# Graph attention with a residual layer norm: adjacency pieces ahead of the other loads, table stores from ScalarE's queue, x tiles from SP's, and beta added two iterations later

## The chip, the cores and the metric

The kernel runs on one core of a Trainium2 chip. Its time is the device time in microseconds of that core; the figure quoted for a kernel is the median of several executions. One further execution is taken with the hardware profiler; its time is given beside the span of the trace.

## The reference, cut to what matters

The input x is 8 batches of 2048 nodes with 64 features (float32), adj a sparse 2048 x 2048 integer matrix. Node n has links to the nodes m with adj[n, m] > 0, and to itself. In the inputs low-numbered nodes have the most links.

```python
def _gat_layer(h, mask, b):
    scores = jnp.einsum('...nd,...md->...nm', h, h)
    scores = jnp.where(mask, scores, NEG)
    attn = jax.nn.softmax(scores, axis=-1)
    return jnp.einsum('...nm,...md->...nd', attn, h) + b

mask = graph + jnp.eye(N, dtype=graph.dtype) > 0
h = jnp.einsum('bnc,hdc->bhnd', x, Wh)                    # 4 heads of 64
out_h = _gat_layer(h, mask[None, None], bh[None, :, None, :])
z = leaky_relu(concat of the heads, 0.2)
h2 = jnp.einsum('bnk,dk->bnd', z, Wo)
out2 = _gat_layer(h2, mask[None], bo)
z2 = leaky_relu(out2, 0.2)
out = (z2 - mean) * rsqrt(var + 1e-5) * gamma + beta
x = layernorm(x + out)
```

## The kernel before, in words

The kernel doesn't compute all 2048 x 2048 scores. The first 32 nodes ("hubs") are treated against all nodes. The other 2016 nodes form 168 sets of 12 nodes; for each set the kernel makes a list of up to 128 nodes that any of the twelve is linked to, fetches their rows by an indirect DMA, and computes scores, softmax and weighted sum on that list alone. The first layer takes two sets an iteration, 84 iterations; the second layer follows on rows stored to a second table. A general kernel stands behind a flag for inputs whose lists don't fit; it doesn't run here.

The work falls into three stages.

**The opening**, a loop over 16 tiles of 128 nodes (`for i in range(NB)`, L977). `load_x(i + 4)` (L469) fetches an x tile with two DMAs, four tiles ahead, into one of ten row buffers. `save_x(i)` (L476) stores tile i in the order of the sets to `table1` in DRAM, with one to five DMAs. `hub_scores(i)`, `turn_x(i + 1)` and `hub_values(i - 1)` are the hubs' attention: per tile a subtract on VectorE (L617), an exponential (L619) and a copy of the transposed tile (L607) on ScalarE, in that order.

Beside it the lists are made. The adjacency rows of ten sets are read in two halves; such a half is a *piece*, 120 rows of 1024 integers, and there are 34 (12 for the first 60 sets, 12 for the next 60, 10 for the rest). `more(n)` issues the next n of them by `load_adj` (L686): two or three DMAs on SP's queue (L693, L694) into one of three `raw` buffers, shared at the start with the two halves of the hubs' own rows, then a conversion on GpSimd (L699) into half of a bf16 tile `a`, and after every second piece four or more small selects (L707, L710). The tiles `a` have five buffers, two of which first hold the hubs' mask. `make_keys(r, t, ...)` (L732) turns three tiles `a` into keys by matmuls with powers of two (L741) and two VectorE operations (L730). `make_keys(0, 0)` comes in tile 2, `make_keys(0, 1)` in tile 6, `make_keys(1, 0)` after the loop, behind the last `hub_values`. From the keys of the first round `pick(0)` makes 39 small VectorE jobs, four a tile from tile 6 on, which end in the lists (`index`).

After the loop come `more(2)`, six gathers from `table1` (`gather`, L813, L816, on GpSimd) and `own_rows` (L819, on GpSimd), whose product the next TensorE work (L831) reads.

**The first layer's loop**, `for i in range(-4, NG + 3)` (L1121), written out by hand as a pipeline: scores (L846), masking (L851), exponential (L858), values (L871), the turn back and the projections. In iteration i the rows for i + 5 are gathered. One more piece is issued per iteration (L1163) until they run out.

In iterations 30 to 73 the kernel also prepares x + beta for the end: `load_own(v)` (L938), 12 DMAs on SP's queue (L946) that bring the x rows of eight sets into one of two buffers `xb`, and `add_beta(v)` (L948), which adds beta on GpSimd (L950) and stores the tile to `table3` from SP's queue (L951). Even iterations load, odd ones add what the iteration before loaded. At the end of each iteration `keep_rows` (L917, L922) stores the finished rows of two sets to the second table, also from SP's queue, from one of four row buffers.

**The second layer** (from L1213) fetches rows of the second table and ends in the layer norms and the stores of the output.

The order of instructions on each engine and each DMA queue is the order in which the code issues them. An instruction on GpSimd, or a DMA on a queue, that waits holds all that was issued after it on the same engine.

Of the kernel before, what the change touches and what calls it, by code (L numbers as in the profile page):

```python
# [359 lines left out]
def fast_kernel(ctx: ExitStack, tc: tile.TileContext, x, adj, Wh, bh, Wo, bo, gamma, beta, out, flag):  # L360


    nc = tc.nc
    B, N, C = x.shape
    H, D, _ = Wh.shape
    P = 128
# [37 lines left out]
    def rows_tile(name):  # L404
        return rowp.tile([P, Q, PW], F32, tag="rows", name=name)
# [25 lines left out]
    NV = (NS + 7) // 8  # L431
# [18 lines left out]
    xrow = {}  # L450
# [10 lines left out]
    def in_order(table, a, b):  # L461

        sets = table[HUB:, :].rearrange("(s k) c -> k s c", k=SET)
        runs = [(0, HUB, table[:HUB, :])]
        runs += [(n0, n0 + n, sets[0, s0:s0 + n]) for s0, n0, n in flipped(0, NS)]
        runs += [(HUB + k * NS, HUB + (k + 1) * NS, sets[k]) for k in range(1, SET)]
        return [(max(a, n0), min(b, n1), dst[max(a, n0) - n0:min(b, n1) - n0]) for n0, n1, dst in runs if max(a, n0) < min(b, n1)]

    def load_x(i):  # L469
        t = xrow[i] = rows_tile(f"x{i}")  # L470
        nc.vector.memset(t[:, :, 0:PW:PW - 1], 1.0)
        for p in range(2):
            nc.scalar.dma_start(out=t[:, :, 1 + p * D:1 + (p + 1) * D],
                                in_=x[p::2, i * P:(i + 1) * P, :].rearrange("q n c -> n q c"))

    def save_x(i):  # L476
        for a, b, dst in in_order(table1, i * P, (i + 1) * P):
            nc.sync.dma_start(out=dst, in_=xrow[i][a - i * P:b - i * P].rearrange("n q c -> n (q c)"))

    NCH = HALFN  # L480
    in_round = [min(FIRST, NS - FIRST * r) for r in range(NR)]
# [116 lines left out]
    def hub_columns():  # L598
        py = two("pyh")
        for h in range(H):  # L600
            nc.tensor.matmul(py[:, 0, h * P:(h + 1) * P], gram[:, h, :], xT[:, :, :HUB], start=True, stop=True)
        nc.vector.tensor_copy(yh.rearrange("p (m h) -> p m h", h=H), py[:, 0, :].rearrange("p (h m) -> p m h", h=H))
# [129 lines left out]
    def make_keys(r, t3, new):  # L732

        n = in_round[r]
        groups = [(t, min(S10, n - S10 * t)) for t in range(3 * t3, min(3 * t3 + 3, (n + S10 - 1) // S10))]
        pk = new(f"pk{r}_{t3}")
        for h in range(2):
            c = (2 * t3 + h) * 32
            for b in range(2):
                for i, (t, ns) in enumerate(groups):  # L740
                    nc.tensor.matmul(pk[c:c + 32, b, :], powers_of(ns, t % 3), ahead[r, t][:ns * SET, h, b * 512:(b + 1) * 512],  # L741
                                     start=(i == 0), stop=(i == len(groups) - 1), tile_position=(0, c))
        for h in range(2):
            part = slice((2 * t3 + h) * 32, (2 * t3 + h + 1) * 32)
            keep_keys(keys[r % 2][part, :], pk[part], part, h)
# [192 lines left out]
    def load_own(v):  # L938
        t = xbs[v % 2]
        if v == NV:  # L940
            for q in range(Q):
                nc.sync.dma_start(out=t[q * HUB:(q + 1) * HUB, :2], in_=x[2 * q:2 * q + 2, :HUB, :].rearrange("p n c -> n p c"))
            return
        for k in range(4):
            for part, src in places(x, v, k):
                nc.sync.dma_start(out=t[part].rearrange("p (f w) c -> p f (w c)", f=2), in_=src)  # L946

    def add_beta(v):  # L948
        t = xbs[v % 2]
        nc.gpsimd.tensor_tensor(t, t, bet.unsqueeze(1).to_broadcast([P, 8, D]), OP.add)  # L950
        nc.sync.dma_start(out=table3[v], in_=t.rearrange("p b d -> p (b d)"))  # L951
# [3 lines left out]
    def more(n):  # L955

        for _ in range(n):
            if pieces:
                load_adj(*pieces.pop(0))

    more(2)
    hub_mask()
    hub_mask_sets()
    weights()
    turn_x(0)
    hub_columns()
    picks = []

    def some(n):
# [7 lines left out]
    for i in range(NB):  # L977
        if i + 4 < NB:
            load_x(i + 4)
        more(2 if i < 5 else 0 if i < 8 else 1)  # L980
        save_x(i)
        if i == 2:
            nc.gpsimd.memset(rall[:, NG:, :], 1.0)
            nc.gpsimd.memset(rall2, 1.0)
            nc.gpsimd.memset(over, 0.0)
            for k in range(SET):
                nc.gpsimd.memset(bits[:, k:k + 1], N << k)
            nc.gpsimd.memset(shifts[:, 2:3], EPS)
            nc.gpsimd.memset(ones, 1.0)
            for t in rowts + xbs:  # L990
                nc.gpsimd.memset(t, 1.0)
            if last:
                make_powers6()
        hub_scores(i)
        if i + 1 < NB:
            turn_x(i + 1)
        if i:
            hub_values(i - 1)
        if i in (2, 6):
            make_keys(0, i // 6, two)  # L1000
            if i == 6:
                picks = pick(0)
        some(4)
# [117 lines left out]
    for i in range(-4, NG + 3):  # L1121
        if 0 <= i + 1 < NG:
            sp = one(f"s{i + 1}", "S")
            scores(i + 1, sp)
            weigh(i + 1, sp)
        if i >= 1 and slow and len(slow) % 3:
            slow.pop(0)()
        cat = one(f"cat{i}", "C") if i <= NG else None
        if i < NG:
            ph, pr = cat[:, 0, 384:384 + GM], cat[:GM, 1, 384:512]  # L1130
        else:
            cat = one(f"cat{i}", "S" if i == NG + 1 else "C")
            ph, pr = cat[:, 0, :GM], cat[:GM, 1, :P]
        if 0 <= i - 1 < NG:
            project(held.pop(("ot", i - 1)), cat, GM)
            held["z", i - 1] = leaky(cat, GM, f"z{i - 1}")
        if 0 <= i + 2 < NG:
            t = held["T", 1, i + 2] = work.tile([P, 2, 512], F32, tag="xTg", name=f"xTg{i + 2}", bufs=3)
            for k in range(2):
                nc.scalar.copy(t[:, k, :], bank[k])  # L1140
        if 0 <= i + 1 < NG:
            lift(i + 1)
        if 0 <= i < NG:
            op = one(f"o{i}", "O")
            values(i, op)
            invert(i, op)
        if 0 <= i + LOOK < NG and i > -3:
            for j in range(2):
                gather(table1, 2 * (i + LOOK) + j, 1, rows_tile)
        if NG - LOOK <= i < NG - 1:  # L1150
            for j in range(2):
                k = 2 * (i - NG + LOOK) + j
                hub_block(k, rows_tile(f"gh{k}"))
        if i + 6 < NG and i % 2 == 0 and i >= -2:
            own_rows((i + 6) // 2)
        if i >= 60 and i % 2 == 0 and ahead_of_second:
            ahead_of_second.pop(0)()
        if 0 <= (i - 30) // 2 <= NV:
            (add_beta if i % 2 else load_own)((i - 30) // 2)
        if 0 <= i - 1 < NG:  # L1160
            leak(held["z", i - 1])
        if i >= -3:
            more(1)  # L1163
        if i >= 0:
            if turns():
                some(1)
            if slow and len(slow) % 3 == 0:
                slow.pop(0)()
            if todo3 and i == todo3[0][0]:
                r, part = todo3.pop(0)[1:]  # L1170
                make_keys(r, part, late_two)
                if part:
                    waiting.append(r)
            if not picks:
                ready = done
                if waiting:
                    r = waiting.pop(0)
                    picks = pick(r)
                    done += in_round[r]
            assert i + 1 + LOOK >= NG or 2 * (i + 1 + LOOK) + 1 < ready  # L1180

        if 0 <= i - 2 < NG:
            second_maps(i - 2, ph)
        if 0 <= i - 3 < NG:
            second_rows(i - 3, pr)
        if 0 <= i + 4 < NG + NG % 2:
            columns(i + 4, cat)
        if 0 <= i - 2 < NG:
            keep_own(i - 2, ph)
        if 0 <= i - 3 < NG:  # L1190
            keep_rows(i - 3, pr)
        for _ in range((2 if i < 22 or i % 2 else 1) if i >= 0 else 0):
            if not turns():
                some(1)
        if 0 <= i + 4 < NG + NG % 2:
            keep_columns(i + 4, cat)
        if 0 <= i + 3 < NG:
            turn(bank[0], rows[1, 2 * (i + 3)])
        if 0 <= i < NG:
            turn_values(i, op)  # L1200
            keep_values(i, op)
        if 0 <= i + 3 < NG:
            turn(bank[1], rows[1, 2 * (i + 3) + 1])
        if NG - 3 <= i < NG:
            hub_step(i - NG + 3, bank[0])
# [205 lines left out]
    for u in range(-3, NU + 5):  # L1411
# [12 lines left out]
        if 0 <= u < NU:  # L1424
            a = u % 2
# [10 lines left out]
        if 0 <= u + 1 < NU:  # L1436
            turn_scores(u + 1)
            a = (u + 1) % 2
# [49 lines left out]
```

## Time and profile before

| | |
|---|---|
| median of 3 runs | 898.96 us (896.56 to 905.24) |
| profiled execution | 1030.36 us, span 1028.6 us |
| mean granted TensorE clock in it | 0.924 |
| busy PE, DVE, ACT, POOL | 784.7, 598.0, 507.6, 501.8 us |
| DMA | 125.70 MB, mean 122 GB/s |

PE is TensorE's matmuls, PEld its weight loads, DVE VectorE, ACT ScalarE, POOL GpSimd, SP the engine that only issues DMAs. SPq and ACTq mark what a sequencer did itself, such as issuing a DMA: start, time the issue took, source line. A line of the timeline has the start and the time in us, then engine, source line, operation, output tile<-inputs, shape and count; in brackets stands how long the engine had been idle before it and what ended that. "issue" is time in which the engine waited for nothing that the profile shows. L537 is a helper's line and stands for all transposes of tiles.

### The profile page before, as it was taken

How to read it: one execution, taken by the hardware profiler on the slowest of the kernel's cores; microseconds unless marked ns; L12 is line 12 of the kernel's file. 1: busy time of each engine (PE TensorE's matmuls, PEld its weight loads, DVE VectorE, ACT ScalarE, POOL GpSimd, SP SyncE). 2: the span in 40 equal slices, each digit the busy share in tenths (PEclk: the TensorE clock that was granted, in tenths of full speed). 3: DMA queues.
4: the chain of work that ended last, by engine and by line, in shares of the span. 5: the costliest groups of instructions: out<-in, count | busy, mean ns of one | idle time of the engine just before them, and what ended most of it. 6: DMA issues, size and time to landing. Idle time of an engine off the chain costs nothing.

```text
span 1028.6 us, 42341 instructions
## 1 busy us (share of the span) xinstructions
PE 784.7 (76%) x18079; PEld 675.7 (66%) x18079; DVE 598.0 (58%) x1358; ACT 507.6 (49%) x1038; POOL 501.8 (49%) x709
## 2 busy tenths in 40 slices
PE   3656588999999999898998997319777667677840
PEld 3535477888998888787887886117666555555740
DVE  2339646888777767544555554001467676657793
ACT  2313145655666656555565673005455655555640
POOL 6342756644545555555565532742455565555100
PEclk9978789999999999999999999559899999999975
DMA  7566634432333434344343432953344555544210
GB/s 162 163 198 167 195 102 139 135 81 75 87 89 103 121 110 120 109 113 117 115 114 110 115 96 79 271 143 95 99 119 132 143 150 143 149 138 141 76 52 25
DMA packets 82419, 125.70 MB, mean 122 GB/s; under 512 B 35440, under 2 KB 51672, under 8 KB 82222
## 3 DMA queue, kind: packets, MB, share of 16 engines
q0 software_dynamic: 27168, 69.09, 25.0%
q1 hardware_dynamic: 37922, 49.47, 15.8%
q10 hardware_dynamic: 17132, 4.34, 2.2%
q8 instruction: 145, 2.38, 1.0%
q14 instruction: 52, 0.43, 0.1%
HBM read 124.98 MB, written 18.48 MB: 139 GB/s over the span
## 4 chain that ended last, share of the span: by engine, by line
PE 61%; DVE 12%; issue 9%; ACT 7%; another core or an unknown queue 4%; DMA 3%; SPq 2%; ACTq 1%; POOL 0%; DVEq 0%; POOLq 0%
PE s L846 11%; PE o L871 9%; PE bank L537 7%; PE t L537 6%; PE cat L831 5%; PE cat L556 3%; PE o L888 3%; PE bank L1239 3%; PE cat L905 3%; ACT xts L1384 2%; PE bank L1250 2%; PE o L1269 2%; PE cat L915 2%; DVE var L1319 1%
## 5 line engine op out<-in xcount | busy, mean ns | idle before, releaser
L816 POOL DMA_INDIRECT g<-table,index x168 | 178.4, 1062 | 158.2 <-PE o L871 127.7
L816 POOL DMA_INDIRECT rows<-table,index x168 | 174.0, 1035 | 148.9 <-PE o L1269 88.7
L851 DVE TENSOR_TENSOR e<-s,mask 128x768 f32<-128x768 f32 x84 | 80.4, 957 | 116.7 <-PE s L846 112.8
L846 PE MATMUL s<-y,xTg 64*64 64x48 f32 x5376 | 122.9, 222 | 22.4 <-issue 20.3
L846 PEld LDWEIGHTS s<-y,xTg 64*64 64x64 f32 x5376 | 103.9, 134 | 45.0 <-issue 41.2
L1384 ACT COPY xts<-t 128x1024 f32<-128x1024 f32 x84 | 81.3, 1011 | 82.4 <-PE t L537 43.8
L543 ACT ACTIVATE z<-cat,bhp 128x192 f32<-128x192 f32 x168 | 61.6, 418 | 95.8 <-PE cat L556 94.0
L537 PE MATMUL t<-ident,rows 128*128 128x128 f32 x672 | 93.9, 285 | 14.0 <-issue 13.4
L537 PE MATMUL bank<-ident,g 128*128 128x128 f32 x672 | 102.2, 276 | 0.4 <-DVE keysi L785 0.3
L871 PE MATMUL o<-g,e 128*64 128x65 f32 x2688 | 100.2, 228 | 1.0 <-issue 1.0
L871 PEld LDWEIGHTS o<-g,e 128*64 128x64 f32 x2688 | 88.1, 141 | 11.5 <-issue 2.0
L537 PEld LDWEIGHTS t<-ident,rows 128*128 128x128 f32 x672 | 78.9, 146 | 22.7 <-issue 21.8
L1140 ACT COPY xTg<-bank 128x512 f32<-128x512 f32 x168 | 90.4, 597 | 1.1 <-PE bank L537 1.0
L537 PEld LDWEIGHTS bank<-ident,g 128*128 128x128 f32 x672 | 81.8, 143 | 2.8 <-DVE keysi L785 0.6
L1239 PE MATMUL bank<-xts,share 128*32 128x128 f32 x1344 | 56.6, 281 | 34.9 <-issue 18.9
L858 ACT ACTIVATE e<-e,shifts 128x768 f32<-128x768 f32 x84 | 81.0, 965 | 3.3 <-DVE e L851 3.3
L837 ACT COPY y<-cat 128x384 f32<-128x384 f32 x80 | 40.9, 511 | 69.5 <-DVE rowt L919 35.1
L699 POOL TENSOR_SCALAR a<-raw 120x1024 bf16<-120x1024 int32 (+1 forms) x34 | 38.0, 1119 | 70.0 <-DMA raw<-in_adj_dram 62.6
L1239 PEld LDWEIGHTS bank<-xts,share 128*32 128x32 f32 x1344 | 38.5, 111 | 50.2 <-issue 45.9
L831 PE MATMUL cat<-xo,gram 128*128 128x192 f32 x320 | 65.7, 328 | 0.0
L878 DVE RECIPROCAL rall<-o 64x8 f32<-64x8 f32 x168 | 34.5, 205 | 48.8 <-PE o L871 47.4
L1269 PE MATMUL o<-rows,share 128*32 128x65 f32 x2688 | 54.6, 228 | 8.5 <-issue 4.6
(193 smaller groups left out, 1469.0 us busy)
## 6 DMA issues: line engine op xcount, KB each, us to landing
raw<-in_adj_dram SPq DMA_DIRECT2D x32, 440.0 KB
table<-xb SPq DMA_DIRECT2D x22, 256.0 KB
xr_s<-table SPq DMA_DIRECT2D x21, 256.0 KB
x<-in_x_dram ACTq DMA_DIRECT2D x32, 128.0 KB
table<-rowt SPq DMA_DIRECT2D x166, 24.4 KB
xb<-in_x_dram SPq DMA_DIRECT2D x168, 22.0 KB
out_dram<-y_s SPq DMA_DIRECT2D x160, 22.0 KB
g<-table,index POOLq DMA_INDIRECT x168
```

The lines of the kernel that those rows point to most:

```text
L537: nc.tensor.transpose(tp[:, q * P:(q + 1) * P], rows[:, q, 1:1 + P], ident)
L543: nc.scalar.activation(z[:, hp], cat[:, :, hp * n:(hp + 1) * n], AF.Identity, bias=bhp[:, hp:hp + 1], scale=1.0)
L816: nc.gpsimd.indirect_dma_start(out=t.rearrange("n q c -> n (q c)"), out_offset=None, in_=table, in_offset=bass.IndirectOffsetOnAxis(ap=ind ...
L831: nc.tensor.matmul(cat[:, k, 2 * GM:2 * GM + n], gram[:, g % 2 * 2 + k, :], held["x", g // 2][:, :n], start=True, stop=True)
L846: nc.tensor.matmul(sp[half(r), p, (q * 2 + j) * M:(q * 2 + j + 1) * M], xt[half(p), j, q, half(r)], y[half(p), (j * Q + q) * M:(j * Q + q ...
L851: nc.vector.tensor_tensor(e[:, :16 * M].rearrange("p (a q n) -> p a q n", a=2, q=Q), sp[:, :, :8 * M].rearrange("p a (q n) -> p a q n", q= ...
L858: nc.scalar.activation(e[:, :16 * M], e[:, :16 * M], AF.Exp, bias=shifts[:, 0:1], scale=1.0)
L871: nc.tensor.matmul(op[half(p), j, o0:o0 + K1], e[:, c0:c0 + 64], rw[j][:, q, sums(p)], start=True, stop=True)
L1140: nc.scalar.copy(t[:, k, :], bank[k])
L1239: nc.tensor.matmul(sp[q * 32:(q + 1) * 32, k, :], bd[u % 3][:, k, q, :], xt[:, s % 2, q, :], start=True, stop=True, tile_position=(0, q * 32))
L1269: nc.tensor.matmul(op[t * 32:(t + 1) * 32, f, k * W2 + p:k * W2 + p + K1], e[:, 2 * q + p, k, :], rw[:, q, sums(p)], start=(a == 0 and k = ...
L1384: nc.scalar.copy(t, tp)
```

## The change

Five edits, all in the order and place of issue; no arithmetic changes.

- `load_x`: tiles 0 to 3 stay on ScalarE's queue, tiles 4 to 15 are issued from SP's.
- `save_x`: the stores to `table1` are issued from ScalarE's queue, not SP's.
- Pieces: six instead of two ahead of `hub_mask`, four more after `hub_columns`, none in tiles 0 to 5 but two after `make_keys` in tile 2, then one a tile from tile 6. Before, two a tile in tiles 0 to 4 and one a tile from tile 8. At the end of the tile loop 20 pieces had been issued before, and 22 are now; `more(2)` after the loop is the same.
- The small memsets on GpSimd that stood in tile 2 stand in tile 3.
- `add_beta(v)` comes three iterations after `load_own(v)`, not one.

```diff
         for p in range(2):
-            nc.scalar.dma_start(out=t[:, :, 1 + p * D:1 + (p + 1) * D],
+            queue = nc.scalar if i < 4 else nc.sync
+            queue.dma_start(out=t[:, :, 1 + p * D:1 + (p + 1) * D],
                                 in_=x[p::2, i * P:(i + 1) * P, :].rearrange("q n c -> n q c"))
...
         for a, b, dst in in_order(table1, i * P, (i + 1) * P):
-            nc.sync.dma_start(out=dst, in_=xrow[i][a - i * P:b - i * P].rearrange("n q c -> n (q c)"))
+            nc.scalar.dma_start(out=dst, in_=xrow[i][a - i * P:b - i * P].rearrange("n q c -> n (q c)"))
...
-    more(2)
+    more(6)
     hub_mask()
     hub_mask_sets()
     weights()
     turn_x(0)
     hub_columns()
+    more(4)
...
         if i + 4 < NB:
             load_x(i + 4)
-        more(2 if i < 5 else 0 if i < 8 else 1)
+        more(1 if i >= 6 else 0)
         save_x(i)
-        if i == 2:
+        if i == 3:
             nc.gpsimd.memset(rall[:, NG:, :], 1.0)
...
             make_keys(0, i // 6, two)
+            if i == 2:
+                more(2)
...
-        if 0 <= (i - 30) // 2 <= NV:
-            (add_beta if i % 2 else load_own)((i - 30) // 2)
+        if i % 2 == 0 and 0 <= (i - 30) // 2 <= NV:
+            load_own((i - 30) // 2)
+        if i % 2 and 0 <= (i - 33) // 2 <= NV:
+            add_beta((i - 33) // 2)
```

## The prediction

> **What bounds the kernel now.** I read the page first, then busy time by stage, then the opening in order of time with its chain of waits, and last the stretch in which beta is added. By stage (length, then busy PE, PEld, DVE, ACT, POOL, clock, DMA share, GB/s):
>
> ```profile
> 0.00:58.40 58.40, 31.66 (x538) 25.54 (x538) 18.11 (x34) 16.96 (x25) 30.34 (x100) 0.97 0.69 165
> 58.40:69.70 11.30, 3.38 (x20) 1.09 (x20) 0.00 (x0) 1.41 (x2) 3.28 (x7) 0.68 0.65 201
> 69.70:117.50 47.80, 30.02 (x611) 24.77 (x612) 44.56 (x119) 14.12 (x17) 16.80 (x34) 0.82 0.64 186
> 117.50:139.00 21.50, 16.26 (x212) 13.28 (x212) 4.99 (x10) 5.55 (x10) 16.34 (x23) 0.69 0.62 173
> 139.00:304.40 165.40, 156.01 (x3876) 136.97 (x3872) 131.13 (x337) 98.62 (x225) 89.50 (x141) 1.00 0.36 97
> 304.40:573.00 268.60, 249.51 (x6175) 222.36 (x6174) 157.83 (x396) 159.27 (x360) 150.22 (x202) 0.98 0.41 114
> ```
>
> The main loop is PE's (156.0 of 165.4 us). The opening is not: a latency chain of about 4.2 us per tile up to 58 us, a hole of 11 us in which DVE does nothing, then DVE at 44.6 of 47.8 us, then POOL at 16.3 of 21.5. The timeline shows what the hole waits for:
>
> ```profile
> 40.09 1.61 PE L741 MATMUL pk<-a,powers 120*32 120x512 bf16 x10 [1.99 <-POOL a L710]
> 54.34 2.18 POOL L699 TENSOR_SCALAR a<-raw 120x1024 bf16<-120x1024 int32 x2
> 57.50 0.37 SPq L693 DMA_DIRECT2D raw<-in_adj_dram  x1
> 65.36 1.08 POOL L699 TENSOR_SCALAR a<-raw 120x1024 bf16<-120x1024 int32 x1 [2.32 <-DMA raw<-in_adj_dram]
> 66.92 2.75 PE L741 MATMUL pk<-a,powers 120*32 120x512 bf16 x10 [7.92 <-POOL a L710]
> ```
>
> make_keys (L741) needs pieces 1 to 6 at tile 2 and 7 to 12 at tile 6. It waited 1.99 us, then 7.92 us for piece 12, converted at 65.36. That piece was issued only at 57.50, when piece 9, whose raw buffer it takes, was converted (54.34), and piece 9 stood on POOL behind the memsets of tile 2 (49.04 to 54.34). The end of the opening:
>
> ```profile
> 114.88 1.14 POOL L699 TENSOR_SCALAR a<-raw 120x1024 bf16<-120x1024 int32 x1 [0.54 <-DMA raw<-in_adj_dram]
> 117.60 1.18 POOL L816 DMA_INDIRECT g<-table,index  x1 [0.17 <-issue]
> 117.44 2.00 PE L630 MATMUL oh<-x,e 128*64 128x65 f32 x32 [3.02 <-ACT e L619]
> 119.37 2.44 PE L741 MATMUL pk<-a,powers 120*32 120x512 bf16 x12
> 126.03 1.65 PE L831 MATMUL cat-4_1517<-xo,gram 128*128 128x192 f32 x4 [4.23 <-issue]
> ```
>
> Six gathers follow piece 22 on POOL from 117.60; own_rows comes after them, and PE's next work (126.03) waits for it. Here POOL is the path. Last, the stretch with load_own and add_beta: values (L871, 32 matmuls an iteration) by windows, and POOL's waits:
>
> ```profile
> 251.80:304.40 52.60, 11.53 (x320) 1.00 0.33 86
> 304.40:336.70 32.30, 6.92 (x192) 1.00 0.39 104
> 336.70:573.00 236.30, 47.92 (x1248) 0.98 0.41 115
> ...
> POOL xb L950 <- DMA table<-rowt: 22.3, 8, 3.4
> POOL xb L950 <- DMA xb<-in_x_dram: 21.6, 11, 3.9
> ```
>
> An iteration takes 5.26 us before load_own starts, 5.38 us in its first six iterations, then 236.3/39 = 6.06 us. PE's own waits in the last window are 16.8 us of "issue" inside L846, none on POOL's or SP's product.
>
> [...] a store L478 costs its queue 0.38 us, a load L473 0.50. [...] an x copy on ACT's queue landed 3.88 us after 28.75, but 8.46 us after 58.67, with pieces and stores in flight on SP's. [...]
>
> **The change, part by part.**
>
> *Pieces ahead, memsets from tile 2 to 3.* Bytes and instructions are the same. Pieces 1 to 10 now stand on SP ahead of x tile 4; 11 and 12 follow make_keys of tile 2. Up to piece 4 (converted 24.4) little moves, since three raw buffers set the order. From there each piece of 0.49 MB takes about 3 us at 165 GB/s and stores come between: 8 x 3.3 puts piece 12 at 51, with its L707 and L710 at 53. Piece 6 is ready near 32 instead of 40.6. Both are ahead of PE (38 and 56.4), so both waits go: 1.99 + 7.92, and the ten matmuls after the hole run in 1.6 instead of 2.75 us (as at 40.09): 11.0. Next late would be x tile 4, now on SP behind piece 10: issued near 35, landing near 41 behind three pieces, needed at 42.3 (44.35 less 2). I take 1 us off (0 to 4). Gain 10, between 7 and 11. After it DVE sets the pace (44.6 of 47.8), so the gain is kept up to the end of the tile loop.
>
> *Two more pieces ahead of the gathers.* The loop after the change takes 10 pieces from tile 6 on, so the two after the loop are 23 and 24, not 21 and 22. The pool of a has five buffers: pieces 13 to 22 fill all five, and 23 needs the one that make_keys(1,0) reads. Its L699 must wait for PE (119.37 + 2.4 in the times of before), and the gathers stand behind it on POOL. From the end of hub_values, 119.44: 2.3 of make_keys, 1.1 for piece 23, 2.56 for piece 24 with its selects (114.88 to 117.44), 0.15: the first gather is 6.1 us after it; before it was 1.84 us ahead. Loss 7.9. If the gathers could have gone as soon as the index stood (112.5), it would be 13; below 7.9 I see no way, because each wait is an in-order one. The pieces then end at iteration 6 instead of 8; PE is the path there: 0, at most 1.
>
> *Stores on ACT, x tiles 4 to 15 on SP.* ACT gets 33 x 0.38 = 12.5 us of issue and loses 24 x 0.50 = 12.0; SP the reverse. On ACT a store follows xT(i) and stands ahead of e(i), which waits over 2 us for DVE anyway (idle 2.5 to 3.3 us before L619), so 0.4 to 0.9 us is hidden. But it can hold ACT if the store must wait for older copies: the chain shows SP's copies at 32.64 and 67.15 released by x copies of the other queue, so the queues are coupled. Unknown: 0 taken, up to 5 lost at the first three tiles, where POOL, PE and DVE all hang on ACT; nothing is gained below 0, as the issue times cancel.
>
> *add_beta two iterations later.* Same instructions. POOL's 44 us of waiting for its loads goes. None of it is on PE's path by name; PE's gathers are five ahead. What it may bring is timing: POOL is free at once, so gathers stay right behind values, as in the first six iterations with load_own (5.38), not 2 to 4 us late and on top of L846. Bounds: 0 if the load's DMAs alone starve PE, (6.06 - 5.38) x 39 = 26 if it is all timing. SP gets a new wait: load_own(v+2) overwrites the buffer whose store was issued one iteration earlier. SP's turn becomes 6.2 (twelve loads) + 1.28 + 0.36 + the store's landing, 2 to 4 by the same kind of copies, so 9.8 to 11.8, against two PE iterations of 10.8 to 12.1. SP's row stores stand behind it with four buffers. Cost 0 to 5. I take +5 net.
>
> Sum: 10 - 7.9 - 0 + 5 = 7 us. The profiled execution took 1030.4 (span 1028.6), the median of the runs 898.96. The difference lies in part in waits like "issue", so I carry over the in-order terms one to one, and took the timing term at a fifth: 898.96 - 7 = 892.
>
> **Rivals.** A, the sum: 892 (887 to 899), within 1%; 0.45. A measurement of this kernel tells about 1%, 9 us, from no change. B, the beta stretch falls to its first pace: 20 of the 26 us plus 2: 877. For it: 5.38 with all loads running. Against: PE names no wait on POOL. 0.33 (880 to 887 with part of it). C, slower: pieces 23 and 24 in front of the gathers. Place: POOL after the tile loop; price 7.9, or 13 where the index had been ready first; it decides as soon as the hole at tile 6 gives less than about 4, which it does if pieces land sooner without the profiler. 13 - 3 = 10: 909. Against: the 5.3 us of memsets ahead of piece 9 are compute and stay in any execution. 0.15. D, the reordering does nothing, since three raw buffers hold the pieces back as before: 899; 0.07.
>
> **How the numbers follow.** Faster by over 1% is B and a corner of A: 0.37. Slower by over 1%: most of C, 0.14. Within: 0.49. Range 876 to 907: B's full size at one end, most of C at the other.
>
> **What would show it.** Right: no idle ahead of L741 at tiles 2 and 6, DVE's keys (L730) of tile 6 near 59 instead of 69.7, the first gather 6 us after hub_values ends, PE idle some 12 us there, and no POOL wait at L950. B shows as under 5.7 us an iteration between 40 and 70 of the loop. Wrong if ACT idles ahead of the stores at tiles 0 to 2, if x tile 4 is waited for by more than 4 us, or if the gathers start ahead of make_keys(1,0).

## The result, and the profile after

The kernel after takes 892.4 us (median of 20 runs, 888.7 to 904.3) against 898.4 us for the kernel before beside it (890.8 to 908.8): a ratio of 0.9934, interval 0.9912 to 0.9956. That is the predicted 892 and "within 1%". The trace shows that it got there by another way.

One thing is needed to read what follows: the level of the times differs between series of runs, and each series was taken on another chip. On the chip of these runs before takes 898 us and on that of the last run below 902, but on the chips of all the other experiments 1031 to 1034, which is the level of the profiled execution that the prediction was read from. (That it is the chip itself that sets the level was not tested.) So kernels are compared by their ratio within one series, and traces only with traces of the same level. The change was therefore run again on a slower chip, where its ratio is 0.9953 (0.9928 to 0.9977), the same gain within the intervals.

Line numbers of after: L473 to L958 of before are one higher (L619 is L620, L741 is L742, L871 is L872); behind that they shift a little more.

The timeline of after on the quicker chip: first four lines of the first tiles, then make_keys of tile 6 and the scores of tile 8, then what follows the tile loop:

```profile
32.78 1.08 POOL L700 TENSOR_SCALAR a<-raw 120x1024 bf16<-120x1024 int32 x1 [5.09 <-DMA raw<-in_adj_dram]
36.14 10.17 ACTq L479 DMA_DIRECT2D table<-x  x5
46.42 1.15 ACT L620 ACTIVATE e<-e,shifts 128x1024 f32<-128x1024 f32 x1 [21.61 <-DMA table<-x]
48.09 1.98 PE L615 MATMUL sh<-share,xT 64*64 64x128 f32 x32 [17.27 <-ACT xT L608]
...
74.40 1.92 PE L742 MATMUL pk<-a,powers 120*32 120x512 bf16 x12
85.51 1.98 PE L615 MATMUL sh<-share,xT 64*64 64x128 f32 x32 [4.88 <-ACT xT L608]
...
124.83 3.28 PE L742 MATMUL pk<-a,powers 120*32 120x512 bf16 x12
127.70 2.13 POOL L700 TENSOR_SCALAR a<-raw 120x1024 bf16<-120x1024 int32 x2 [8.86 <-PE pk L742]
130.98 1.12 POOL L817 DMA_INDIRECT g<-table,index  x1 [0.30 <-DVE rall L638]
139.35 1.65 PE L832 MATMUL cat-4_1538<-xo,gram 128*128 128x192 f32 x4 [11.24 <-POOL xo L826]
```

ScalarE stands idle for 21.6 us ahead of the exponential of tile 0, because the five stores that come before it in ScalarE's order can't be issued (the first goes out at 36.14), and PE waits 17.3 us for ScalarE. That is the largest single event of the opening, and the forecast had 0 to 5 us there. The hole at tile 6 is gone (L742 has no bracket); the next scores wait 4.9 us, for ScalarE behind DVE's work on the keys. Pieces 23 and 24 wait for make_keys(1,0), and PE idles 11.2 us, as predicted.

The stages of the two kernels on chips of the same (slower) level, all read from their traces:

| | before | after | difference |
|---|---|---|---|
| hub_scores of tile 1 start | 30.3 | 48.8 | +18.5 |
| last hub_values end | 118.7 | 125.3 | +6.5 |
| first gather | 114.9 | 131.3 | +16.4 |
| PE's next work (L831, L832) | 123.4 | 139.7 | +16.3 |
| values of iteration 0 | 137.7 | 152.9 | +15.2 |
| values of iterations 0 to 83 | 486.8 | 467.7 | -19.1 |
| behind values of iteration 83 | 404.9 | 406.4 | +1.5 |
| span | 1029.4 | 1027.0 | -2.4 |

The opening doesn't gain 2 us, it loses 15. The first layer's loop gains 19. Busy time of 39 iterations, from values of iteration 36 to those of 75 (length, then busy PE, PEld, DVE, ACT, POOL, clock, DMA share, GB/s), before:

```profile
345.45:584.09 238.64, 218.13 (x5348) 193.56 (x5345) 130.35 (x323) 137.71 (x312) 133.70 (x176) 0.99 0.40 113
```

and after on the same level:

```profile
362.18:580.01 217.83, 210.29 (x5348) 188.08 (x5345) 131.93 (x323) 139.25 (x312) 131.19 (x176) 1.00 0.44 124
```

The matmuls are the same; their length falls from 238.6/39 = 6.12 to 217.8/39 = 5.59 us an iteration. PE is idle 20.5 us in the first and 7.5 in the second (length less busy), and its busy time falls by another 7.8.

### The profile page after: what moved, and what is told of

It reads as the page before. It is cut to its first block, busy times and chain, and to the rows that moved or that the text cites. A ratio compares the mean times of both kernels' runs of the same rounds, so it can differ in the third digit from the quotient of the medians.

```text
span 890.9 us, 42340 instructions
## 1 busy us (share of the span) xinstructions
PE 729.4 (82%) x18079; PEld 644.2 (72%) x18079; DVE 592.2 (66%) x1358; ACT 502.6 (56%) x1038; POOL 503.2 (56%) x709
## 3 DMA queue, kind: packets, MB, share of 16 engines
q1 hardware_dynamic: 48088, 48.36, 18.6%
## 4 chain that ended last, share of the span: by engine, by line
PE 52%; DVE 16%; DMA 13%; issue 6%; SPq 5%; ACT 4%; POOL 2%; ACTq 0%; POOLq 0%; DVEq 0%
PE o L872 10%; PE s L847 9%; PE bank L538 7%; DMA raw<-in_adj_dram 6%; PE cat L832 5%; PE cat L557 3%; PE o L889 3%; SPq L1358 3%; DMA rows<-table,index 3%; PE cat L906 3%; PE t L538 2%; PE cat L916 2%; DVE st_s L1309 2%; DVE y_s L1329 2%; DMA table<-x 2%
## 5 line engine op out<-in xcount | busy, mean ns | idle before, releaser
L817 POOL DMA_INDIRECT rows<-table,index x168 | 178.1, 1060 | 55.5 <-issue 23.2
L872 PE MATMUL o<-g,e 128*64 128x65 f32 x2688 | 100.5, 226 | 4.7 <-issue 4.5
L872 PEld LDWEIGHTS o<-g,e 128*64 128x64 f32 x2688 | 87.3, 139 | 16.1 <-issue 6.2
L847 PE MATMUL s<-y,xTg 64*64 64x48 f32 x5376 | 97.6, 221 | 1.3 <-DVE share L731 1.2
L847 PEld LDWEIGHTS s<-y,xTg 64*64 64x64 f32 x5376 | 86.9, 135 | 15.6 <-issue 15.1
L538 PE MATMUL t<-ident,rows 128*128 128x128 f32 x672 | 86.3, 279 | 10.1 <-DMA rows<-table,index 9.4
L538 PEld LDWEIGHTS t<-ident,rows 128*128 128x128 f32 x672 | 76.5, 144 | 14.2 <-issue 6.3
L832 PE MATMUL cat<-xo,gram 128*128 128x192 f32 x320 | 65.9, 328 | 0.7 <-issue 0.7
L880 DVE TENSOR_TENSOR osb<-o,rall 128x512 f32<-128x512 f32 x84 | 58.1, 692 | 2.9
L620 ACT ACTIVATE e<-e,shifts 128x1024 f32<-128x1024 f32 x16 | 18.4, 1149 | 73.2 <-DVE e L618 36.1
L832 PEld LDWEIGHTS cat<-xo,gram 128*128 128x128 f32 x320 | 53.3, 201 | 1.6 <-issue 1.4
## 6 DMA issues: line engine op xcount, KB each, us to landing
table<-rowt SPq DMA_DIRECT2D x166, 24.4 KB
```

The lines of the kernel that those rows point to most:

```text
L538: nc.tensor.transpose(tp[:, q * P:(q + 1) * P], rows[:, q, 1:1 + P], ident)
L817: nc.gpsimd.indirect_dma_start(out=t.rearrange("n q c -> n (q c)"), out_offset=None, in_=table, in_offset=bass.IndirectOffsetOnAxis(ap=ind ...
L832: nc.tensor.matmul(cat[:, k, 2 * GM:2 * GM + n], gram[:, g % 2 * 2 + k, :], held["x", g // 2][:, :n], start=True, stop=True)
L847: nc.tensor.matmul(sp[half(r), p, (q * 2 + j) * M:(q * 2 + j + 1) * M], xt[half(p), j, q, half(r)], y[half(p), (j * Q + q) * M:(j * Q + q ...
L872: nc.tensor.matmul(op[half(p), j, o0:o0 + K1], e[:, c0:c0 + 64], rw[j][:, q, sums(p)], start=True, stop=True)
L880: nc.vector.tensor_tensor(osb, v[:, :, :, 1:K1], r.unsqueeze(3).to_broadcast([P, 4, 2, D]), OP.mult)
```

## The experiments

**The kernel before, profiled again.** No edit.

> The kernel before, unchanged, profiled once more, because the profiled execution that the prediction was read from took 1030.4 us where the runs took 899. The theory on record assumes that the in-order terms (7.92 and 1.99 us ahead of L741, the gathers 1.84 us ahead of the end of hub_values) and the 6.06 us per iteration after load_own starts stand in any execution: they should come back within 1 us, and within 0.2 us per iteration. The rival: the 6.06 us belonged to that one execution, and then the loop runs at 5.3 to 5.5 us in this one and moving add_beta has little to win.

Measured: 1031.2 us, span 1029.4. PE's waits in tiles 2 and 6:

```profile
38.93 1.60 PE L741 MATMUL pk<-a,powers 120*32 120x512 bf16 x10 [0.31 <-POOL a L710]
...
66.32 1.90 PE L741 MATMUL pk<-a,powers 120*32 120x512 bf16 x8 [8.47 <-POOL a L710]
```

The hole at tile 6 and the 6.1 us an iteration come back. The wait at tile 2 is 0.31 here, not 1.99, and the first gather is 3.9 us ahead of the end of hub_values, not 1.84. So terms of the prediction's sum varied by 2 us from one execution to the next; they had been expected back within 1.

**The two halves of the change.** First add_beta alone:

```diff
-        if 0 <= (i - 30) // 2 <= NV:
-            (add_beta if i % 2 else load_own)((i - 30) // 2)
+        if i % 2 == 0 and 0 <= (i - 30) // 2 <= NV:
+            load_own((i - 30) // 2)
+        if i % 2 and 0 <= (i - 33) // 2 <= NV:
+            add_beta((i - 33) // 2)
```

> Only add_beta is moved; the opening is that of before. The theory on record (opening gains 2, add_beta 5): about 893, 5 us under before. The theory that the trace after suggests (the opening loses some 13 us, because ACT stands 21.6 us in front of its first stores, and the main loop, at 5.3 us an iteration instead of 6.06, pays for it): about 880, 18 to 20 us under before, faster than the whole change. Third: add_beta does nothing (898) and the gain of 6 us comes from somewhere in the opening or behind it.

Measured: 1015.3 against 1032.6, ratio 0.9831 (0.9787 to 0.9875): 17 us. Then everything but that:

> All of the change but add_beta, which is issued where it was before. The theory on record: 2 us under before, 896. The theory from the trace after: the opening alone costs 13 us, 911. Third (the opening wins, add_beta nothing): 892.

Measured: 1047.5, ratio 1.0113 (1.0054 to 1.0172): 12 us slower than before by the ratio. Its six runs lie in two groups, near 1037 and near 1049, so the size is known only to within the interval, 6 to 18 us. And the whole on a chip of the same level:

> The kernel after, unchanged, on the chip of the other runs, so that its stages stand beside theirs. If the parts add: moving add_beta alone gave 1015.3 against 1032.6 (17.3 less), the rest alone 1047.5 (11.7 more by the ratio of 1.0113), so the whole is 5 to 6 us under before. Values of iteration 0 then start near 151.4, as without add_beta, and iterations 36 to 74 take 5.65 us as with add_beta alone. If the parts interact (a late opening leaves more pieces in the loop), another sum.

Measured: 1026.0 against 1033.7, ratio 0.9953 (0.9928 to 0.9977). The parts multiply to 0.9831 x 1.0113 = 0.9942, inside that interval, so as far as the runs can tell they add. The prediction's two sums, 2 us for the opening and 5 for add_beta, are both wrong by more than 10 us and in opposite directions. This split was measured on the slower chips alone; on the quicker kind only the whole change and the last kernel below were run.

**Whose wait add_beta removes.** In the trace of before that was taken again, from about iteration 30 to 75, POOL and SP both wait at add_beta (engine, line, what was waited for: us in total, times, longest). POOL, whose wait for values (the first line) is the normal one:

```profile
POOL g L816 <- PE o L871: 55.0, 29, 3.2
POOL xb L950 <- DMA table<-rowt: 33.3, 11, 3.8
...
POOL xb L950 <- DMA xb<-in_x_dram: 9.7, 4, 2.9
```

and SP's queue, which holds the store L951 behind that addition, with the row stores and the next loads behind it:

```profile
SPq L951 <- POOL own L911: 23.6, 13, 4.4
SPq L951 <- DMA xb<-in_x_dram: 20.2, 19, 1.5
SPq L951 <- POOL xb L950: 13.5, 9, 1.6
```

With add_beta moved alone, POOL no longer waits there, but for values, as it should:

```profile
POOL g L816 <- PE o L871: 88.2, 45, 3.0
POOL g L816 <- issue: 10.3, 28, 2.1
```

Two kernels separate the two. In the first, the addition stays where it was and only the store goes later:

```diff
     t = xbs[v % 2]
     nc.gpsimd.tensor_tensor(t, t, bet.unsqueeze(1).to_broadcast([P, 8, D]), OP.add)
-    nc.sync.dma_start(out=table3[v], in_=t.rearrange("p b d -> p (b d)"))
+def save_beta(v):
+    nc.sync.dma_start(out=table3[v], in_=xbs[v % 2].rearrange("p b d -> p (b d)"))
...
+        if i % 2 and 0 <= (i - 33) // 2 <= NV:
+            save_beta((i - 33) // 2)
```

> The kernel before, with the addition of beta where it was (one iteration after its loads, so POOL waits for them as before) and only its store on SP two iterations later. If it is POOL's waiting that costs the 17 us (43 us at the addition in the loop, with the gathers and own behind it): no gain, 1030 to 1033, iterations 36 to 74 at 6.1 us. If it is SP, whose store waits for POOL's addition with the row stores and the next loads behind it: about 1015, at 5.65 us.

Measured: 1023.1, ratio 0.9919 (0.9891 to 0.9947), 5.81 us an iteration. Its POOL still waits:

```profile
POOL xb L950 <- DMA table<-rowt: 18.6, 8, 3.8
...
POOL xb L950 <- DMA xb<-in_x_dram: 11.1, 6, 3.3
POOL xb L950 <- issue: 6.6, 3, 3.1
```

In the second the addition is left out and the store stays in place:

```diff
-        nc.gpsimd.tensor_tensor(t, t, bet.unsqueeze(1).to_broadcast([P, 8, D]), OP.add)
```

> The kernel before without the addition of beta (left out of the result); the store stands where it was, so SP itself waits there for the loads to land, and POOL waits for nothing. If it is POOL's waiting that costs: about 1015, iterations 36 to 74 at 5.65 us, or a little under, as the addition itself is gone too (22 times). If it is SP's: 1030 or so, at 6.1 us.

Measured: 1013.4, ratio 0.9834 (0.9769 to 0.99), 5.61 us an iteration. SP, expected to wait there as long as before, waited 3.0 us in total:

```profile
SPq L950 <- DMA xb<-in_x_dram: 3.0, 7, 1.3
```

So this kernel did not hold SP up and can't acquit SP; it shows that without the addition both waits vanish. The first kernel does tell them apart, and neither theory has it whole: freeing SP alone brings 0.81% of the 1.69%, freeing POOL as well brings the rest. That is about half each by the medians; the iterations of the profiled executions (6.12, 5.81 and 5.64 us) give SP two thirds. With the intervals of both ratios SP's share may lie anywhere from a quarter to nearly nine tenths. That each of the two has a part is shown, how large it is isn't.

**The queues swapped back.** After, with stores on SP and x tiles on ScalarE's queue as in before:

```diff
-            queue = nc.scalar if i < 4 else nc.sync
-            queue.dma_start(out=t[:, :, 1 + p * D:1 + (p + 1) * D],
+            nc.scalar.dma_start(out=t[:, :, 1 + p * D:1 + (p + 1) * D],
...
-            nc.scalar.dma_start(out=dst, in_=xrow[i][a - i * P:b - i * P].rearrange("n q c -> n (q c)"))
+            nc.sync.dma_start(out=dst, in_=xrow[i][a - i * P:b - i * P].rearrange("n q c -> n (q c)"))
```

> The whole change but the two queues: stores on SP again, x tiles on ACT again; pieces, memsets, pieces 23 and 24 and add_beta as after. The theory on record, in which the swap of queues costs nothing: 892, the same as after. The theory from the trace after, in which stores on ACT's queue hold ACT up behind pieces: ACT is not idle 21.6 us ahead of e of tile 0, and the time falls by about 13 to 15, to 878. Third: with the stores on SP they stand behind ten pieces in order instead, x tiles and stores come late all the same, and it is not faster than after (892 to 900).

Measured: 1029.3, ratio 0.9973 (0.9953 to 0.9994), not told apart from after. ScalarE's waits from 14 to 60 us in this kernel, whose line numbers here are those of before:

```profile
ACT e L619 <- DMA x<-in_x_dram: 19.0, 1, 19.0
...
ACT e L619 <- DMA raw<-in_adj_dram: 6.3, 1, 6.3
```

The theory that the stores on ScalarE's queue are at fault falls. Now it is the x tile that ScalarE issues at tile 0 that can't be issued, and ScalarE stands for 19.0 us instead of 21.6. In both kernels what ScalarE issues behind the ten pieces of SP's queue is held, be it stores (the first goes out at 36.14) or an x tile (37.71).

**The pieces in before's turn.** After, but the pieces two at the start and then two a tile; queues, memsets at tile 3 and add_beta as after:

```diff
-    more(6)
+    more(2)
     hub_mask()
...
-    more(4)
...
-        more(1 if i >= 6 else 0)
+        more(2 if i < 5 else 0 if i < 8 else 1)
...
-            if i == 2:
-                more(2)
```

> The kernel after with the pieces issued in before's turn (two at the start, two at a tile up to tile 4, none to tile 7, then one); stores on ACT, x tiles on SP, memsets at tile 3 and add_beta late all stay. If it is the pieces ahead that hold up the other copies: ACT is not idle 21.6 us ahead of e of tile 0, the scores of tile 1 start near 31 instead of 48, the first gather is ahead of the end of hub_values again, and the time is 17 us of add_beta and a few of the memsets under before, 1006 to 1015. If it is the stores on ACT's queue: tile 1 stays late by 10 us or more, and it ends at 1025 or above.

Measured: 1012.6, ratio 0.9831 (0.9753 to 0.9909). Tile 1 starts at 30.2, and values of iteration 0 at 138.3, where before has 137.7 and after 152.9. This is add_beta's 0.9831 again: the swapped queues and the memsets at tile 3 are worth nothing that these four runs can tell (their interval is 8 us wide on either side). The order of the pieces, with the two more that it puts ahead of the gathers, is the loss.

**hub_mask ahead of the pieces.** Why do pieces that are issued first hold the rest? In after the first five are converted at 14.3, 20.4, 26.6, 32.8 and 39.6, 6.1 to 6.8 us apart, though there are three raw buffers: piece 2 is issued at 15.44, only when piece 1 is converted. Two of the three buffers hold the hubs' own rows, which hub_mask reads, and six pieces were put ahead of hub_mask. In time hub_mask is early (its two reads start at 3.66 and 4.97 us in after), so what counts would be its place in the order of the code:

```diff
-    more(6)
     hub_mask()
+    more(6)
     hub_mask_sets()
```

> The kernel after with one line moved: hub_mask is issued ahead of the first six pieces instead of behind them. The two copies of the hubs' rows take two of the three raw buffers until hub_mask; in after the pieces stand ahead of it, so pieces 1 to 5 seem to go one by one through the third buffer, 6.2 us each (converted at 14.3, 20.4, 26.6, 32.8, 39.6). If that is the cause: from piece 2 on they come 2 to 4 us apart, piece 5 is converted near 28 instead of 39.6, the first e is late by 5 to 10 us instead of 18, and the time falls by 8 to 13 from after's 1026, to 1013 to 1018. If ten pieces ahead of the stores are too much by their bytes alone (4.9 MB at some 165 GB/s is 30 us): the first e still near 42 to 46, and the time within 4 us of after, 1022 to 1030.

Measured: 1014.4, ratio 0.9836 (0.979 to 0.9882), 1.2% under after by one line. Pieces 2 to 5 and the first exponential:

```profile
18.02 1.09 POOL L700 TENSOR_SCALAR a<-raw 120x1024 bf16<-120x1024 int32 x1 [2.95 <-DMA raw<-in_adj_dram]
21.07 1.09 POOL L700 TENSOR_SCALAR a<-raw 120x1024 bf16<-120x1024 int32 x1 [1.08 <-DMA raw<-in_adj_dram]
23.58 1.11 POOL L700 TENSOR_SCALAR a<-raw 120x1024 bf16<-120x1024 int32 x1 [1.42 <-DMA raw<-in_adj_dram]
26.05 1.09 POOL L700 TENSOR_SCALAR a<-raw 120x1024 bf16<-120x1024 int32 x1 [0.50 <-DMA raw<-in_adj_dram]
...
31.82 1.15 ACT L620 ACTIVATE e<-e,shifts 128x1024 f32<-128x1024 f32 x1 [6.35 <-DVE x L471]
...
59.81 1.92 PE L742 MATMUL pk<-a,powers 120*32 120x512 bf16 x12
```

Piece 5 comes at 26.05, the first exponential only 3.1 us later than in before (28.7), and make_keys of tile 6 runs at 59.8 without a wait; in before it ended its wait at 66.3. The last hub_values end at 110.3, 8.4 us ahead of before's 118.7. This is the tile loop that the prediction described. The opening as a whole still gains nothing on before: values of iteration 0 start at 137.5 (137.7 in before), because pieces 23 and 24 take the 8.4 us back.

How pieces that come one by one hold a copy on another queue was not tested by itself. In after's trace the wait of the first store, which goes out at 36.14, ends with the landing, at 36.12, of a copy of piece 5 that SP's queue had issued at 34.20; why the one waits for the other is not shown.

**Pieces 23 and 24 behind the gathers.** After, with

```diff
     make_keys(1, 0, two)
-    more(2)
...
     own_rows(1)
+    more(2)
```

> The kernel after with the two pieces behind the tile loop (23 and 24) moved behind the first six gathers and own_rows. By the prediction's step they cost 7.9 us, at most 13 where the index stands first; the traces show the first gather at 131.3 (after, same chip) and PE's next work at 139.7, 14.5 behind the end of hub_values, against 4.7 in before. If they cost what was predicted: first gather near 121 to 124, values of iteration 0 7 to 9 us earlier, 1017 to 1019. If PE is held by something else there (the late stores of the table, which the gathers need): no gather before 128, and within 3 us of after. If the late pieces hold up make_keys in the loop, the gain is given back by iteration 14.

Measured: 1021.1, ratio 0.9891 (0.9847 to 0.9936). The first gather is at 125.2, 6.1 us earlier than in after, and values of iteration 0 at 146.9, 6.0 earlier, a little less than the 7 to 9 expected. The interval overlaps that of after, so the trace, of one execution, carries this one.

**The memsets later.** The kernel with pieces in turn, memsets at tile 5 instead of 3:

```diff
-        if i == 3:
+        if i == 5:
             nc.gpsimd.memset(rall[:, NG:, :], 1.0)
```

> Pieces in turn as in the last call's fourth kernel (1012.6), and the memsets not at tile 3 but at tile 5, behind piece 12. At tile 2 or 3 they stand ahead of piece 9 or 11, and make_keys of tile 6 waits some 8 us for piece 12. If the memsets make that wait: the keys of tile 6 come 4 to 8 us earlier and it ends near 1006. If the pieces' bytes do (piece 12 lands late whatever POOL does): within 2 us of 1012.6.

Measured: 1014.6, ratio 0.9835 (0.9797 to 0.9873): nothing. Its wait at tile 6, with all memsets behind piece 12:

```profile
66.60 2.75 PE L742 MATMUL pk<-a,powers 120*32 120x512 bf16 x10 [6.85 <-POOL a L711]
```

Piece 12 was converted at 65.04, against 63.96 with the memsets at tile 3. So the hole isn't the memsets'. (The profiled execution took 1025.1 us; the same wait is 7.33 us in the trace with the memsets at tile 3.) What POOL waits for there is the pieces' loads, 3.83 us ahead of piece 11 (converted at 61.12) and 2.84 us ahead of piece 12; what makes them late in this kernel is not shown. In the trace of before that the prediction was read from, SP's queue stands:

```profile
49.07 0.84 SPq L694 DMA_DIRECT2D raw<-in_adj_dram  x1
55.63 0.36 SPq L478 DMA_DIRECT2D table<-x  x1
56.09 0.35 SPq L693 DMA_DIRECT2D raw<-in_adj_dram  x1
```

There a store of SP's queue stands 5.7 us for an x copy of ScalarE's queue that landed at 55.61, and pieces 11 (56.09) and 12 (57.50) stand behind that store. It is one queue waiting for a copy of the other again, as after's first store does at 36.14.

**Both mends.**

```diff
-    more(6)
     hub_mask()
+    more(6)
...
     make_keys(1, 0, two)
-    more(2)
...
     own_rows(1)
+    more(2)
```

> The kernel after with both mends: hub_mask ahead of the first six pieces, and pieces 23 and 24 behind the first gathers and own_rows. Each alone took 12 and 5 us from after (1014.4 and 1021.1 against 1026.0). With hub_mask first the tile loop ends 8 us earlier than in before (end of hub_values 110.3), but the first gather was still at 115.9, behind make_keys(1,0) and pieces 23 and 24. If the two add: first gather near 110, values of iteration 0 near 131, and 1007 to 1010. If the index, which DVE makes at the end of the loop, holds the gathers as late as the pieces did: first gather at 113 or later and 1011 to 1015.

Measured: 874.1 against 902.4 (this chip is of the quicker level), ratio 0.9693 (0.9636 to 0.9751). That beats both kernels: 28 us under before, where after is 6 under, and it is more than the 12 and 5 us that the single mends took from after on the slower chips, added to those 6. First gather and the work behind it:

```profile
107.19 1.12 POOL L817 DMA_INDIRECT g<-table,index  x1 [2.88 <-DVE member L799]
...
110.76 3.52 PE L742 MATMUL pk<-a,powers 120*32 120x512 bf16 x12
...
115.56 0.92 PE L832 MATMUL cat-4_1538<-xo,gram 128*128 128x192 f32 x4 [1.28 <-POOL xo L826]
```

The gathers now wait 2.88 us for DVE's lists alone and start 3.6 us ahead of the end of hub_values; PE's 11.2 us of idle are 1.3. Against the trace of after on a chip of this level (span 890.9), values of iteration 0 start at 125.9 instead of 150.2, 24.3 us earlier; the span is 867.7, 23.2 shorter. With hub_mask first the gathers go 3.6 us ahead of the end of hub_values, with pieces 23 and 24 moved alone only 0.3: the two pieces had more to hold up once the opening was mended.

## Why the prediction was right, point by point

The number and the class were right, by luck; the account behind them was not. Two errors of more than 10 us cancelled: the opening was put at a gain of 2 and lost 12 to 15, add_beta at a gain of 5 and it brought 17 to 19.

*Pieces ahead.* The failed step is "up to piece 4 (converted 24.4) little moves, since three raw buffers set the order". Piece 4 was converted at 32.8. There were not three buffers for the pieces but one, as long as hub_mask stood behind them in the code; the kernel's description above even says that the hubs' rows share the buffers. With hub_mask moved ahead the rest of that step held: no waits at tiles 2 and 6, the matmuls of the keys at 59.8, and 8.4 us gained by the end of the tile loop where 7 to 11 had been said. In after itself the same repairs can be seen: the delay of 18.5 us at tile 1 is 6.5 at the end of hub_values, so 12 were won back.

*Its reason.* The prediction read the hole as piece 12 waiting for piece 9, and piece 9 for the memsets; "the 5.3 us of memsets ahead of piece 9 are compute and stay in any execution". As a cause that is false: moving the memsets changed nothing (tested with the queues as in after). The trace that it was read from has SP's queue standing until 55.63 ahead of pieces 11 and 12, for a copy of the other queue.

*Stores on ScalarE's queue.* "0 taken, up to 5 lost at the first three tiles": it was the right place with the wrong size and, in part, the wrong culprit. The prediction had even seen in the chain that copies of SP's queue (at 32.64 and 67.15) were released by x copies of ScalarE's, but set the price at 0, its author's estimate from the issue times alone. The loss is 17 us of waiting PE, it comes with the pieces, and swapping the queues back does not remove it. The swap as such is not told apart from nothing: after without it measures 0.9973 of before (0.9953 to 0.9994), after itself 0.9953 (0.9928 to 0.9977). The prediction's own sign for being wrong, ScalarE idle ahead of the stores, is what the trace shows first.

*Pieces 23 and 24.* Right. The first gather comes 6.1 us behind hub_values (130.98 less 124.9), as worked out, and PE idles 11.2 where 12 was said. The loss of 7.9 was near: taking them away gave 6.0 us in after, where POOL then waits 4.3 us for other things. With the opening mended, the stretch from the end of hub_values to values of iteration 0 shrinks from 25.3 to 15.1 us (150.2 - 124.9 and 125.9 - 110.8, chips of one level), 10.3 us. "Below 7.9 I see no way" holds in the second case and misses the first by 2.

*add_beta.* Rival B was right in place and size, within the range (0 to 26): iterations 36 to 74 fall from 6.12 to 5.64 us with this edit alone, 18.6 us of the 26. Its reason, that late gathers lie on top of L846, no run shows. The step that failed is the choice, "+5 net". It read "PE names no wait on POOL" as evidence against; PE's idle time is booked as "issue" inside L846, and moving a wait on two other engines took it from 20.5 to 9.3 us (220.07 less 210.78 in the window below). The cost feared on SP is there (L946 waits 16.2 us in all for table3's store with add_beta moved) and costs nothing that shows. That a part of the gain is SP's, not POOL's, was not in the prediction.

```profile
349.65:569.72 220.07, 210.78 (x5349) 188.41 (x5345) 131.08 (x323) 139.02 (x312) 131.35 (x176) 1.00 0.43 122
```

Rival C named the right place and a part of the loss; rival D's idea, that raw buffers hold the pieces back, was nearest to the cause, but it took the three buffers for granted and so priced it at nothing. What stays open: why PE's "issue" time in L846, and its busy time with it, depend on when POOL and SP are free. The iterations show it, no view says by what.

## What to carry to other kernels

When loads are moved ahead, look at what still occupies the buffers that they rotate through at that point of the program: the last reader of an older tile must be issued ahead of them, or several buffers act as one (here the pieces came 6.1 to 6.8 us apart, and 2.5 to 3.1 with hub_mask ahead of them). Price such a move for every copy issued after it, on the other queue too, since one that can't be issued holds the engine that issues it (here ScalarE, for 21.6 us). A wait on an engine that nobody names as a releaser can still be worth moving (here 17 us). Try each part of a change by itself, because the sum of two unknowns can come out right for no reason.

## What the runs showed of the hardware that was not expected

The same kernel after has a span of 890.9 us on one chip and 1027.0 on another at mean granted clocks of 0.953 and 0.933. Of the 136 us, 114 lie behind the values of iteration 83 (292.1 and 406.4); in the loop an undisturbed iteration (18 to 27) is 5.00 us on the one and 5.23 to 5.32 on the other. The granted clocks differ by 2%, the spans by 15%, so the clock alone doesn't account for it. PE's idle time ahead of the scores' matmuls, most of it "issue", is long only on the slower one; first the quicker one, then the slower (busy us, mean ns of one, idle us before them):

```profile
L847 PE MATMUL s<-y,xTg 64*64 64x48 f32 x5376 | 97.6, 221 | 1.3 <-DVE share L731 1.2
L847 PE MATMUL s<-y,xTg 64*64 64x48 f32 x5376 | 118.5, 222 | 10.0 <-issue 7.7 <-DVE share L731 1.2
```

What makes the difference no run shows. The ratio of the change was the same within the intervals on both, 0.9934 and 0.9953.
